# A transformer block in float32 on one core: the first feed-forward unit formed from seven block products, the first load in two transfers, the last output in columns of 384 and 128

## The chip, the core and the metric

The kernel runs on one core of one Trainium2 chip. The core has a matrix engine (PE, with its weight loads as PEld), a vector engine (DVE), a scalar engine (ACT), GpSimd (POOL) and a queue engine (SP) that only issues transfers. Each engine takes its own instructions in the order in which the built program holds them; engines wait for one another by semaphores. Matrix results go to PSUM, seven banks of 128 x 512 float32 that are used in rotation here (an eighth holds the attention output). The metric is the device time of one execution in microseconds, given as the median of some runs; a profiled execution has its own time, and its span runs from the first to the last instruction.

## The reference

For each of 8 batch entries there are 128 rows of 512 features (x) and 2048 context rows of 384 features. In short:

```
x = x + xattn(layernorm(x), ctx)              # 8 heads of 64; scores over 2048 context rows
h = layernorm(x)
q, k, v = h Wq + bq, h Wk + bk, h Wv + bv
x = x + h + (softmax over the query axis of (q k^T, causal) / sqrt(512)) v
h = layernorm(x)
hid = float8_e4m3(relu(h w1^T + b1))          # 512 -> 2048
x = x + float16(hid float8_e4m3(w2)^T + float16(b2))
```

## The kernel before, in words

**Stages.** The kernel first loads the first context block and the key weights and computes the keys of entry 0 by plain products (`k_plain`, L380), then goes through the eight entries of the cross-attention (keys and values by a scheme with fewer block products, scores, exponentials, transposition, weighted values), then the self-attention in two groups of four entries (`sa0`, `sa1`), and last the feed-forward part, also in two groups of 512 rows (`NG` = 2, `GT` = 512). It is the start, the passage from `sa1` to the feed-forward part, and the end that the change touches.

**Start.** Key weights arrive by six transfers on ACT's queue (L211), the first half of the first context block by six on SP's queue (L218): `n` picks 512 context rows, `k` one of three blocks of 128 features. Seven small products with the identity (L215, `early`) run on PE before any of it is there. Transfers of the two queues draw on eight semaphores in turn; a queue waits for the transfer that used the semaphore before.

**Feed-forward.** A hidden block is 128 hidden units for 512 rows. Computed directly (`hidden`, L1013), it takes four accumulating products (`k`) of 128 x 128 weights with 512 columns; in float32 each shows in the trace as two passes. `FourBlocks` (L1054) computes four hidden blocks at once from a 2 x 2 split of rows and features: seven block products in place of eight. It needs sums of weight blocks (`form_w`, L1034: t1, t2, t3, less_t4, two feature halves each, for a range of block pairs) and sums of row blocks (`form_x`, L1041: s1 to s4), both on DVE. `begin` holds products 1 and 2, `middle` 3 to 5, `end` 6 and 7; each `product` is eight passes with 256 columns. In the kernel before, hidden blocks 0 to 3 of group 0 are computed directly, one ahead of the last two `read` calls of the self-attention and three after them; seven `FourBlocks` units follow. The output (`output`, L1112, float8 weights; `finish`, L1119) of group 0 is put between the units of group 1; group 1's comes at the end, its last entry in two halves of 256 columns (L1189).

**What sets the order.** PE's order is written by hand for the whole kernel. ACT's and DVE's is written by hand up to L1155 and L1156 (`first.close()`, `in_turn.close()`): instructions emitted inside that region keep the order of the code. What is emitted after it (`form_x`, `form_w`, `quantize_w2` here) is placed by the build among the others, also ahead of them, by its own estimate of when operands are there.

**Weights w1.** One transfer of 4 MB on SP (L998), issued once the cross-attention's buffers are given up (L991) and the last `project` has been multiplied; the 16 transfers of `w2` (L1008, two buffers) stand behind it. All of w1 is one tile with one semaphore; `form_w` and the hidden products read it.

**The last steps of the self-attention** (L1128 to L1154), for `two` = entries 4 and 5 and then for 6 and 7: `values` is a product into a bank that DVE empties with the bias added (`sv`, L765); `logits` a product that DVE reads with the mask (`lg`, L735) and whose maximum it takes (`snm`, L739); `exps` an ACT step; `probabilities` two small DVE steps (`sr`, `e`); `keys` four products (`psk`) that ACT empties; `read` a product (`pr`) that DVE adds to the rows (L783). `turned_rows` transposes the normalized rows of group 0 on PE (`pt_f`) and copies them on ACT (`xf`).

Of the kernel before, what the change touches and what calls it, by code (L numbers as in the profile page):

```python
# [15 lines left out]
AF = mybir.ActivationFunctionType  # L16
# [4 lines left out]
P = 128  # L21
# [4 lines left out]
def tile_perceiver_block(  # L26
# [21 lines left out]
    nc = tc.nc  # L48
    B, S, D = x.shape
    _, DC, J = ctx_t.shape  # L50
# [5 lines left out]
    NK = D // P  # L56
    NKC = DC // P
    NJ = J // 512
    NJT = J // P
    NHC = HID // P  # L60
    NG = 2
    TMPB = 2
    BK = 256
    EARLY = 7
    GB = B // NG
    GT = GB * S
# [18 lines left out]
    def bank(name):  # L85
        return ps_one.tile([P, 512], F32, tag="bank", name=name)
# [3 lines left out]
    def turned_into(xt, b, xn, name):  # L90

        pt = bank(f"pt_{name}_{b}")
        for k in range(NK):
            nc.tensor.transpose(pt[:, ts(k, P)], xn[:, ts(k, P)], ident)
        nc.scalar.copy(xt[:, :, ts(b % GB, P)], pt.rearrange("p (k t) -> p k t", k=NK))
# [25 lines left out]
    x_both = ctxp.tile([P, 2, NKC, 4, BK], F32, tag="x_both", name="x_both")  # L121
# [91 lines left out]
    early = bank("early")  # L213
    for _ in range(EARLY):
        nc.tensor.matmul(early[:, :P], ident, ident, start=True, stop=True)  # L215
    for n in range(2):
        for k in range(NKC):
            nc.sync.dma_start(  # L218
                x_both[:, 0, k, 2 * n : 2 * n + 2],
                ctx_t[0, ts(k, P), ts(n, 512)].rearrange("p (i j) -> p i j", i=2),  # L220
            )
# [79 lines left out]
    wk4 = wk.rearrange("p k (f j n) -> p k f j n", f=2, j=2)  # L301
# [75 lines left out]
    def k_tile(b, f2):  # L377
        kts[b, f2] = ktp.tile([P, 2, J], F32, tag=f"kt{f2}", name=f"kt_{b}_{f2}")

    def k_plain(f2):  # L380


        k_tile(0, f2)
        for n in range(2):
            pss = [bank(f"k_{f2}_{j}_{n}") for j in range(2)]
            for k in range(NKC):
                for j in range(2):
                    nc.tensor.matmul(  # L388
                        pss[j], wk4[:, k, f2, j, :], x_both[:, 0, k, 2 * n : 2 * n + 2],
                        start=(k == 0), stop=(k == NKC - 1),  # L390
                    )
                if (n, k) == (1, 0):
                    yield
            for j in range(2):
                nc.scalar.copy(kts[0, f2][:, j, ts(n, 512)], pss[j])
# [268 lines left out]
    def load_columns(pool, src, name):  # L664
        t = pool.tile(list(src.shape), F32, tag=name, name=name)
        nc.gpsimd.dma_start(t, src)
        return t
# [118 lines left out]
    def all_of(unit):  # L786
        for _ in unit:
            pass
# [71 lines left out]
    def group_stats(g):  # L860

        st = small.tile([P, GB, 6], F32, tag="qst", name=f"fst_{g}")
        mv = small.tile([P, GB, 2], F32, tag="qmv", name=f"fmv_{g}")
        sd = small.tile([P, GB], F32, tag="qsd", name=f"fsd_{g}")
        for i in range(GB):
            nc.vector.bn_stats(st[:, i], xs[g * GB + i])
        for i in range(GB):
            nc.vector.bn_aggr(mv[:, i], st[:, i])
        nc.scalar.activation(sd, mv[:, :, 1], AF.Sqrt, bias=eps)
        return mv, sd  # L870

    def normed_group(g, mv, sd):
        rs = small.tile([P, GB], F32, tag="qrs", name=f"frs_{g}")
        nc.vector.reciprocal(rs, sd)
        out = []
        for i in range(GB):
            xn = sap.tile([P, D], F32, tag="xn", name=f"xn_f_{g}_{i}", bufs=GB + 1)
            nc.vector.tensor_scalar(
                xn, xs[g * GB + i], mv[:, i, 0:1], rs[:, i : i + 1], ALU.subtract, ALU.mult
            )  # L880
            out.append(xn)
        return out

    def turned_rows(g, rows, tag):

        xt = sap.tile([P, NK, GT], F32, tag=tag, name=f"xf_{g}")
        for i, xn in enumerate(rows):
            turned_into(xt, g * GB + i, xn, "f")
        return xt
# [107 lines left out]
    w1 = wff.tile([P, NK, HID], F32, tag="w1", name="w1")  # L997
    nc.sync.dma_start(w1, w1_t.rearrange("(k p) n -> p k n", p=P))  # L998
    b2r = load_row(wff, b2, "b2r")
    b1c = load_columns(wff, b1, "b1c")  # L1000
# [3 lines left out]
    def quantize_w2():  # L1004
        nc.vector.tensor_copy(b2q, b2r)
        for c in range(NHC):
            w = tp.tile([P, D], F32, tag="w2f", name=f"w2f_{c}", bufs=2)
            nc.sync.dma_start(w, w2_t[ts(c, P), :])  # L1008
            nc.vector.tensor_copy(w2[:, c, :], w, saturate=False)

    hq = wff.tile([P, NHC, B * S], E4M3, tag="hq", name="hq")

    def hidden(g, xt, blocks):  # L1013

        for c in blocks:
            ps = bank(f"ph_{g}_{c}")
            for k in range(NK):
                nc.tensor.matmul(  # L1018
                    ps, w1[:, k, ts(c, P)], xt[:, k, :], start=(k == 0), stop=(k == NK - 1)
                )  # L1020
            nc.scalar.activation(hq[:, c, ts(g, GT)], ps, AF.Relu, bias=b1c[:, c : c + 1], saturate=False)

# [4 lines left out]
    def b_of(k, j):  # L1030

        return w1.rearrange("p (q k) (c j n) -> p q k c j n", k=2, j=2, n=P)[:, :, k, :, j]

    def form_w(pairs):  # L1034
        t1, t2, t3, less_t4 = (w_forms[:, i, :, pairs] for i in range(4))
        b11, b12, b21, b22 = (b_of(k, j)[:, :, pairs] for k in range(2) for j in range(2))
        for q in range(2):
            for to, one, two in ((t1, b12, b11), (t2, b22, t1), (t3, b22, b12), (less_t4, b21, t2)):
                nc.vector.tensor_tensor(to[:, q], one[:, q], two[:, q], ALU.subtract)

    def form_x(g, xt):  # L1041
        a = xt.rearrange("p (q k) (i r) -> p q k i r", k=2, i=2)
        a11, a12, a21, a22 = (a[:, :, k, i] for i in range(2) for k in range(2))

        home, tag = ((sap, "sk"), (wff, "x_forms"))[g]
        f = home.tile([P, 4, 2, HR], F32, tag=tag, name=f"x_forms_{g}")
        s1, s2, s3, s4 = (f[:, i] for i in range(4))
        nc.vector.tensor_tensor(s1, a21, a22, ALU.add)
        nc.vector.tensor_tensor(s2, s1, a11, ALU.subtract)
        nc.vector.tensor_tensor(s3, a11, a21, ALU.subtract)  # L1050
        nc.vector.tensor_tensor(s4, a12, s2, ALU.subtract)
        x_forms[g] = a11, a12, a22, s1, s2, s3, s4
# [59 lines left out]
    def output(b, ps, blocks, cols=slice(0, D)):  # L1112
        for c in blocks:
            nc.tensor.matmul(  # L1114
                ps[:, cols], hq[:, c, ts(b, S)], w2[:, c, cols],
                start=(c == 0), stop=(c == NHC - 1),
            )

    def finish(b, ps, cols=slice(0, D)):  # L1119
        n = cols.stop - cols.start  # L1120
        q = tp.tile([P, n], E5M10, tag="q", name=f"q_{b}_{cols.start}", bufs=2)
        nc.vector.tensor_tensor(q, ps[:, cols], b2q[:, cols], ALU.add)
        y = sap.tile([P, n], F32, tag="xn", name=f"y_{b}_{cols.start}", bufs=GB + 1)
        nc.vector.tensor_tensor(y, q, xs[b][:, cols], ALU.add)
        nc.sync.dma_start(out[b][:, cols], y)
# [3 lines left out]
    sa1.scale(B - 1)  # L1129
    sa1.norm(B - 1)  # L1130
    nc.scalar.activation(warm, eps, AF.Exp)
    sa1.values(B - 2)

    sa1.logits(two[0])
# [6 lines left out]
        sa1.probabilities(r)  # L1141
    all_of(sa1.keys(sa1.rows[2:]))
    xfs = [turned_rows(0, xf0, "xt0")]
    for r in sa1.rows[2:]:
        sa1.logits(r)
        sa1.exps(r)
    for r in sa1.rows[2:]:
        sa1.probabilities(r)
    for r in two:
        sa1.read(r)  # L1150

    hidden(0, xfs[0], range(1))
    for r in sa1.rows[2:]:
        sa1.read(r)  # L1154
    first.close()  # L1155
    in_turn.close()  # L1156


    form_x(0, xfs[0])
    form_w(slice(2, 4))  # L1160
    hidden(0, xfs[0], range(1, 4))
    form_w(slice(4, 8))
    quantize_w2()
    form_w(slice(0, 2))
    work = [FourBlocks(0, d) for d in range(1, 4)] + [FourBlocks(1, d) for d in range(4)]
    work[0].begin()
    for i, unit in enumerate(work):
        if i == 1:
            xfs.append(turned_rows(1, normed_group(1, *group_stats(1)), "xt1"))
            form_x(1, xfs[1])  # L1170
        unit.middle()
        if i + 1 < len(work):
            work[i + 1].begin()
            unit.end()
        if i > 2:

            b = i - 3
            ps = bank(f"pf_{b}")
            output(b, ps, range(NHC))
            finish(b, ps)  # L1180
    unit.end()

    pss = [bank(f"pf_{b}") for b in range(GB, B - 1)]
    for b, ps in enumerate(pss, GB):
        output(b, ps, range(NHC - 4))
    for b, ps in enumerate(pss, GB):
        output(b, ps, range(NHC - 4, NHC))
        finish(b, ps)
    for i in range(2):  # L1189
        ps = bank(f"pf_{B - 1}_{i}")  # L1190
        cols = slice(i * D // 2, (i + 1) * D // 2)
        output(B - 1, ps, range(NHC), cols)
        finish(B - 1, ps, cols)

# [46 lines left out]
```

## Time and profile before

| | us |
|---|---|
| median of 3 runs (1086.44 to 1087.02) | 1086.88 |
| profiled execution | 1086.38 |
| its span | 1084.6 |
| PE busy in the span | 1077.8 |
| first `k_plain` pass begins | 4.98 |
| first direct hidden block begins on PE | 950.96 |
| first `FourBlocks` product begins | 966.41 |
| last output product begins its stretch of 80 passes | 1066.58 |

The page gives each engine's busy time and share; a timeline row gives start, duration, engine, line, operation, output tile <- input tiles, shape and count, and in brackets how long the engine stood idle before the row and what ended that. Rows of one line that follow each other are merged. The durations of products are longer than their distance, since passes are pipelined: eight passes with 256 columns are listed as 1.89 us but follow each other every 1.73 us.

### The profile page before, as it was taken

The numbers are of one execution on the slowest core, as the hardware profiler recorded it, in microseconds if no ns is written. First come the engines' busy times: TensorE is split into PE (matmuls) and PEld (weight loads), VectorE is DVE, ScalarE is ACT, GpSimd is POOL, SyncE is SP. The second block draws the span as 40 slices with busy tenths as digits, with TensorE's granted clock in tenths as the row PEclk, the third lists the DMA queues.
The fourth block names the chain that finished last, engine by engine and source line by source line (L and its number), as shares of the span: only waits on it lengthen the run. The fifth ranks groups of instructions, "written<-read, shape, count | busy, mean of one in ns | idle before, by whom it ended". The sixth has DMA issues, their size and how long they took to land.

```text
span 1084.6 us, 15566 instructions
## 1 busy us (share of the span) xinstructions
PE 1077.8 (99%) x5638; PEld 708.4 (65%) x5638; DVE 759.1 (70%) x1639; ACT 352.4 (32%) x559; POOL 234.4 (22%) x350
## 2 busy tenths in 40 slices
PE   9999999999999999999999999999999999999998
PEld 5475774576467647755775577557746656768875
DVE  5876567778777877787688777777877657584333
ACT  3322133324332423432343324332433222323221
POOL 0144130350055005500540153035000312000000
PEclk9999999999999999999999999999999999999999
DMA  9476334553565456536544553555345745431001
GB/s 324 141 188 151 119 78 98 136 147 85 131 155 134 93 136 152 138 87 150 149 100 100 154 146 78 117 137 146 79 112 115 233 122 146 175 106 31 10 17 52
DMA packets 71853, 134.75 MB, mean 124 GB/s; under 512 B 28241, under 2 KB 36449, under 8 KB 70753
## 3 DMA queue, kind: packets, MB, share of 16 engines
q1 hardware_dynamic: 61120, 113.03, 40.8%
q0 software_dynamic: 3312, 11.03, 3.3%
q10 hardware_dynamic: 7344, 9.70, 3.1%
q8 instruction: 45, 0.74, 0.3%
q14 instruction: 32, 0.25, 0.1%
HBM read 54.01 MB, written 10.49 MB: 59 GB/s over the span
## 4 chain that ended last, share of the span: by engine, by line
PE 99%; DMA 0%; ACT 0%; DVE 0%; issue 0%; ACTq 0%
PE pv_z L428 22%; PE pk_z L405 21%; PE po L559 11%; PE sc L504 11%; PE pv_b L428 4%; PE pk_b L405 3%; PE ph_b L1066 3%; PE psk L715 3%; PE psv L759 3%; PE pf L1114 3%; PE pq L472 3%; PE py L642 3%; PE ph_c L1066 2%; PE ph_a L1066 2%; PE k L388 2%; PE ph L1018 1%
## 5 line engine op out<-in xcount | busy, mean ns | idle before, releaser
L528 ACT ACTIVATE p<-p,nm 128x2048 f32<-128x2048 f32 x64 | 128.2, 2003 | 274.9 <-DVE nm L516 185.9
L541 DVE STREAM_TRANSPOSE p<-p 128x512 f32<-128x512 f32 x256 | 158.9, 679 | 62.3 <-ACT p L528 62.1
L508 DVE TENSOR_SCALAR_CACHE_REDUCE p<-sc 128x512 f32<-128x512 f32 x256 | 159.0, 686 | 20.6 <-PE sc L504 18.9
L428 PE MATMUL pv_z<-wv_sums,x_both 128*128 128x256 f32 x640 | 157.9, 381 | 0.0
L165 POOL TENSOR_TENSOR m_both<-x_both 128x256 f32<-128x256 f32 x70 | 51.0, 729 | 490.5 <-DMA x_both<-in_ctx_t_dram 303.1
L405 PE MATMUL pk_z<-x_both,wk_sums 128*128 128x512 f32 (+1 forms) x320 | 149.2, 572 | 1.1 <-ACT kt L325 0.6
L428 PEld LDWEIGHTS pv_z<-wv_sums,x_both 128*128 128x128 f32 x640 | 120.5, 190 | 18.6 <-issue 2.2
L559 PEld LDWEIGHTS po<-pT,v 128*64 128x64 f32 x2048 | 111.2, 137 | 23.9 <-issue 23.2
L559 PE MATMUL po<-pT,v 128*64 128x128 f32 x2048 | 118.9, 274 | 0.1
L504 PE MATMUL sc<-kt,q 64*128 64x512 f32 x512 | 118.5, 602 | 0.0
L428 PE MATMUL pv_z<-wv_sums,m_both 128*128 128x256 f32 x448 | 107.3, 379 | 0.0
L405 PEld LDWEIGHTS pk_z<-x_both,wk_sums 128*128 128x128 f32 x320 | 59.2, 190 | 67.3 <-issue 54.5
L405 PE MATMUL pk_z<-m_both,wk_sums 128*128 128x512 f32 (+1 forms) x224 | 101.4, 568 | 0.0
L428 PEld LDWEIGHTS pv_z<-wv_sums,m_both 128*128 128x128 f32 x448 | 83.4, 190 | 12.6 <-issue 0.6
L504 PEld LDWEIGHTS sc<-kt,q 64*128 64x128 f32 x512 | 46.9, 186 | 65.6 <-issue 54.7
L325 ACT COPY v<-pv_z 128x512 f32<-128x512 f32 x112 | 62.9, 589 | 56.0 <-PE pv_z L428 55.5
L325 ACT COPY kt<-pk_z 128x512 f32<-128x512 f32 (+1 forms) x112 | 59.7, 562 | 58.0 <-PE pk_z L405 57.6
L405 PEld LDWEIGHTS pk_z<-m_both,wk_sums 128*128 128x128 f32 x224 | 40.8, 190 | 46.8 <-issue 35.1
L165 POOL TENSOR_TENSOR x_both<-x_both 128x256 f32<-128x256 f32 x98 | 70.1, 731 | 2.4 <-DMA x_both<-in_ctx_t_dram 2.3
L328 DVE TENSOR_TENSOR v<-pv_z,v 128x512 f32<-128x512 f32 x96 | 63.1, 684 | 5.5 <-PE pv_z L428 5.5
L328 DVE TENSOR_TENSOR kt<-pk_z,kt 128x512 f32<-128x512 f32 (+1 forms) x96 | 59.9, 650 | 5.8 <-PE pk_z L405 5.4
L328 DVE TENSOR_TENSOR v<-pv_b,v 128x512 f32<-128x512 f32 x48 | 32.9, 686 | 40.4 <-PE pv_b L428 40.4
(208 smaller groups left out, 1235.7 us busy)
## 6 DMA issues: line engine op xcount, KB each, us to landing
pT<-p SPq DMA_DIRECT2D x488, 128.0 KB, 2.3
x_both<-in_ctx_t_dram SPq DMA_DIRECT2D x45, 512.0 KB, 5.2
w<-in_w_t_dram SPq DMA_DIRECT2D x1, 4096.0 KB, 12.9
w2f<-in_w_t_dram SPq DMA_DIRECT2D x16, 256.0 KB, 2.7
pT<-p POOLq DMA_DIRECT2D x24, 128.0 KB, 4.1
x_in<-in_x_dram SPq DMA_DIRECT2D x8, 256.0 KB, 7.2
qd<-xq SPq DMA_DIRECT2D x8, 256.0 KB, 2.6
q<-qd SPq DMA_DIRECT2D x8, 256.0 KB, 3.9
```

The lines of the kernel that those rows point to most:

```text
L165: eng.tensor_tensor(x_block(b, h, to), x_block(b, h, one), x_block(b, h, two), ALU.add if op == "+" else ALU.subtract,)
L325: nc.scalar.copy(outs[ij], views(ps))
L328: nc.vector.tensor_tensor(outs[to], views(ps), outs[other], op)
L405: nc.tensor.matmul(ps[:, : n * BK], wk_sums[:, WSLOT[WAT[r]], f2, :], x_block(b, hs, XAT[r]), start=start, stop=True, skip_group_check=True,)
L428: nc.tensor.matmul(ps[:, ts(t, 256)], x[:, ts(t, P)], wv_sums[:, WSLOT[WAT[r]], :], start=start and t == 0, stop=True, skip_group_check=True,)
L472: nc.tensor.matmul(ps, wq[:, k, ts(m, P)], xt[:, k, :], start=(k == 0), stop=(k == NK - 1),)
L504: nc.tensor.matmul(pair[i], q[r, :], kts[b, m // 2][r, m % 2, ts(n, 512)], start=True, stop=True)
L508: nc.vector.tensor_scalar(p[:, :, i].rearrange("p g (t i) -> p t g i", i=SQ)[:, ts(n, Q)], pair[i].rearrange("p (t g i) -> p t g i", g=Q, ...
L528: nc.scalar.activation(p[:, :, i], p[:, :, i], AF.Exp, bias=nms[b, m][:, i : i + 1], scale=SCALE, accum_out=sums[b][:, h : h + 1],)
L541: nc.vector.transpose(p[:, g, i], p[:, g, i])
L559: nc.tensor.matmul(pos[b][h * DH : (h + 1) * DH, ts(m, P)].rearrange("p (a i) -> p a i", a=Q), v[:, jt % 8, ts(2 * m + h, DH)], turned_[b, ...
L1066: nc.tensor.matmul(self.ps[to][:, ts(t, HR)], w[:, q, 2 * self.d + t], x[:, q], start=start and t == q == 0, stop=True, skip_group_check=True,
```

## The change

**1. First unit.** `hidden` is gone. All eight units of the two groups are `FourBlocks`. `form_w(slice(0, 2))` moves from behind `quantize_w2` to the place right after the `warm` activation, ahead of `sa1.values(B - 2)`; `form_x(0, ...)` moves from behind the closing of the region to right after `turned_rows`; the first unit's `begin` stands where hidden block 0 stood, between the two pairs of `read`. The other `form_w` calls and `quantize_w2` stay behind the region.

**2. First load.** The first context transfer (128 x 512) becomes two of 128 x 256, and the four passes of `k_plain` that read it become eight with 256 columns.

**3. Last output.** The last entry's columns are split 384 and 128 in place of 256 and 256.

```diff
-    for n in range(2):
-        for k in range(NKC):
+    for i in range(2):
+        nc.sync.dma_start(x_both[:, 0, 0, i], ctx_t[0, ts(0, P), ts(i, BK)])
+    for n in range(2):
+        for k in range(n == 0, NKC):
...
-                for j in range(2):
-                    nc.tensor.matmul(
-                        pss[j], wk4[:, k, f2, j, :], x_both[:, 0, k, 2 * n : 2 * n + 2],
-                        start=(k == 0), stop=(k == NKC - 1),
-                    )
+                for i in range(2 if f2 == n == k == 0 else 1):
+                    for j in range(2):
+                        to, of = slice(0, 512), slice(2 * n, 2 * n + 2)
+                        if f2 == n == k == 0:
+                            to, of = ts(i, BK), slice(i, i + 1)
+                        nc.tensor.matmul(
+                            pss[j][:, to], wk4[:, k, f2, j, :], x_both[:, 0, k, of],
+                            start=(k == i == 0), stop=(k == NKC - 1), skip_group_check=True,
+                        )
...
     nc.scalar.activation(warm, eps, AF.Exp)
+    form_w(slice(0, 2))
     sa1.values(B - 2)
...
     xfs = [turned_rows(0, xf0, "xt0")]
+    form_x(0, xfs[0])
...
-    hidden(0, xfs[0], range(1))
+    work = [FourBlocks(g, d) for g in range(NG) for d in range(NHC // 4)]
+    work[0].begin()
     for r in sa1.rows[2:]:
         sa1.read(r)
     first.close()
     in_turn.close()
-    form_x(0, xfs[0])
     form_w(slice(2, 4))
-    hidden(0, xfs[0], range(1, 4))
     form_w(slice(4, 8))
     quantize_w2()
-    form_w(slice(0, 2))
-    work = [FourBlocks(0, d) for d in range(1, 4)] + [FourBlocks(1, d) for d in range(4)]
-    work[0].begin()
...
-    for i in range(2):
+    for i, cols in enumerate((slice(0, D - P), slice(D - P, D))):
         ps = bank(f"pf_{B - 1}_{i}")
-        cols = slice(i * D // 2, (i + 1) * D // 2)
         output(B - 1, ps, range(NHC), cols)
```

The built programs differ on PE, DVE, ACT and SP at these places alone. DVE's order in the stretch, as built ("w" is one step of `form_w`, short with 256 columns and long with 512; "s" one of `form_x`; "cast" one block of `w2`; a number is the batch entry):

```
before: ... c_rows, sv6, lg4, snm4, lg5, snm5, sv7, sr4, e4, sr5, e5,
        8 w short, 4 w long, lg6, w long, snm6, lg7, s1, snm7, sr6, s2, e6, sr7, s3, e7,
        rows4, rows5, s4, 2 w long, rows6, rows7, w long, ...
after:  ... c_rows, 10 w short, sv6, lg4, w, snm4, lg5, w, snm5, sv7, sr4, w, e4, sr5, w, e5, 2 w,
        7 w long, s1, w long, s2, s3, s4, lg6, cast, snm6, lg7, cast, snm7, sr6, e6, sr7, e7,
        rows4, rows5, u2, rows6, rows7, ...
```

PE's order in the same stretch, with `psk` the key blocks of entries 6 and 7, and the PSUM banks as the build gave them: before, `psk` 2 takes the bank of `sv6`'s product and `psk` 3 that of `lg4`'s; after, `psk` 2 takes the bank of a transposition that ACT empties, `psk` 3 that of `sv6`'s product, and the four `pt_f` those of `lg4`, `lg5`, `sv7` and of `psk` 0.

```
before: psv6, pl4, pt_s7, pl5, psv7, psk 0-3, pt_f 0-3, pl6, pl7, pr4, pr5, hidden block 0, pr6, pr7, hidden blocks 1-3, ph_a ...
after:  psv6, pl4, pt_s7, pl5, psv7, psk 0-3, pt_f 0-3, pl6, pl7, pr4, pr5, ph_a, ph_b, pr6, pr7, ph_c ...
```

More of the change, by code (lines that the diff above doesn't have):

```diff
@@ L1011, in tile_perceiver_block @@
     hq = wff.tile([P, NHC, B * S], E4M3, tag="hq", name="hq")
[L1013 to L1021, printed above, removed]
     HR = GT // 2
@@ L1156, in tile_perceiver_block @@
     in_turn.close()
-    form_x(0, xfs[0])
     form_w(slice(2, 4))
-    hidden(0, xfs[0], range(1, 4))
     form_w(slice(4, 8))
     quantize_w2()
-    form_w(slice(0, 2))
-    work = [FourBlocks(0, d) for d in range(1, 4)] + [FourBlocks(1, d) for d in range(4)]
-    work[0].begin()
     for i, unit in enumerate(work):
-        if i == 1:
+        if i == 2:
             xfs.append(turned_rows(1, normed_group(1, *group_stats(1)), "xt1"))
@@ L1174, in tile_perceiver_block @@
             unit.end()
-        if i > 2:
-            b = i - 3
+        if i >= GB:
+            b = i - GB
             ps = bank(f"pf_{b}")
```

## The prediction

> **What bounds the kernel now.** I read the page's totals and its chain first, then the list of waits of PE alone, then the timelines of PE and DVE around the edit.
>
> ```profile
> span 1084.6 us, 15566 instructions
> ...
> PE 1077.8 (99%) x5638; PEld 708.4 (65%) x5638; DVE 759.1 (70%) x1639; ACT 352.4 (32%) x559; POOL 234.4 (22%) x350
> ...
> PE 99%; DMA 0%; ACT 0%; DVE 0%; issue 0%; ACTq 0%
> ```
>
> PE is busy for all but 6.8 us of the span, and those lie at the two ends (4.98 - 3.36 us before the first key pass, some 4 us after the last output pass). PE's waits name only two of 0.6 and 0.5 us in between. So PE work taken out shortens the kernel by its whole length, and any pause given to PE lengthens it by its whole length.
>
> ```profile
> 938.80 7.07 PE L715 MATMUL psk<-xt,both 128*128 128x256 f32 x32
> 945.71 1.91 PE L94 MATMUL pt_f<-ident,xn_f 128*128 128x128 f32 x16
> 947.45 1.95 PE L730 MATMUL pl<-xt,sk 128*128 128x128 f32 x16
> 949.24 1.88 PE L782 MATMUL pr<-sv,e 128*128 128x512 f32 x4
> 950.96 3.60 PE L1018 MATMUL ph<-xf,w 128*128 128x512 f32 x8
> 954.39 1.88 PE L782 MATMUL pr<-sv,e 128*128 128x512 f32 x4
> 956.11 10.46 PE L1018 MATMUL ph<-xf,w 128*128 128x512 f32 x24
> 966.41 1.89 PE L1066 MATMUL ph_a<-xf,w 128*128 128x256 f32 x8
> 968.13 1.89 PE L1066 MATMUL ph_b<-x_forms,w_forms 128*128 128x256 f32 x8
> ```
>
> The starts give the prices on PE: a direct hidden block 3.43 us (954.39 - 950.96), a `FourBlocks` product 1.73 us (968.13 - 966.41; 1.727 over the units), a key block 1.73, the four transpositions 1.74, two logits 1.79, two reads 1.72.
>
> ```profile
> 934.81 0.68 DVE L765 TENSOR_TENSOR sv<-psv,bv 128x512 f32<-128x512 f32 x1
> 935.41 0.34 DVE L735 SCALAR_TENSOR_TENSOR lg<-pl,c_rows,mask 128x128 f32<-128x128 f32 x1
> ...
> 939.00 0.69 DVE L765 TENSOR_TENSOR sv<-psv,bv 128x512 f32<-128x512 f32 x1 [2.36 <-PE psv L759]
> ...
> 943.06 0.76 DVE L1039 TENSOR_TENSOR w_forms<-w 128x256 f32<-128x256 f32 x2 [2.58 <-DMA w2f<-in_w_t_dram]
> ```
>
> This is the key view. Before, DVE finishes the softmax steps of entries 4 and 5 and only then waits for w1: the first `form_w` step begins at 943.06. The wait is put down to `w2f`, but w1 is what these steps read, and its issue row says the same: issued at 929.86, and
>
> ```profile
> w<-in_w_t_dram SPq DMA_DIRECT2D x1, 4096.0 KB, 12.9
> ```
>
> which is a landing at 942.8. The first `w2f` block was issued at 930.3 and took 13.1, too late to have ended the wait.
>
> **Part 1, what it saves.** Four direct blocks (4 x 3.43 = 13.73 us) go, seven products (7 x 1.727 = 12.09) come: -1.64 us of PE work. ACT's and DVE's extra evictions for the unit (one copy, eight short activations, four additions) run beside the products, as in the other seven units, which show PE without a pause.
>
> **Part 1, the wait that it adds.** `form_w(slice(0, 2))` now stands inside the hand-ordered region, right behind `c_rows`, which DVE reaches at 934.8. The transfer is issued as before, behind the last `project`, so DVE stands from 934.9 to 943.06. Queued behind the waiting step are `sv6`, `lg4`, `lg5`, `sv7` and everything after; waiting for those are PSUM banks. I follow them with durations of this trace (distance from start to start on DVE: short step 0.336, long step 0.60, `sv` 0.60, `lg` 0.27, `snm` 0.20, `sr` 0.09, `e` 0.20).
>
> First pause. Ten short steps come first: 943.06 + 10 x 0.336 = 946.42; `sv6` ends 0.68 later, 947.10. PE runs on unhindered through `psk` 0 to 2 (938.80 to 943.99); `psk` 3 needs the bank that `sv6` empties, and starts at 947.2 with 0.1 for the signal: **3.2 us** of pause.
>
> Second pause. From 947.2 PE has `psk` 3, transpositions, logits, reads and ph_a: 1.73 + 1.74 + 1.79 + 1.72 + 1.73 = 8.71, till 955.9. ph_b needs s2. DVE from 946.42: two `sv` 1.20, two `lg` and two `snm` 0.94, two `sr` and `e` 0.58, six short steps 2.02, eight long ones 4.82, s1 and s2 (with its end) 1.28: 10.84, so s2 is there at 957.26. Pause **1.4 us**; ph_b ends near 959.1. (ACT, behind DVE by its own queue, copies `xf` by 953, earlier than s1's turn.)
>
> Third pause. `read` 6 needs e6. After s2: s3, s4 1.2; `lg6`, cast, `snm6`, `lg7`, cast, `snm7` 1.6; then `sr6`, `e6` 0.4: near 960.4. PE could start at 959.1 and starts at 960.5: **1.4 us**. `read` 7 and e7 follow without a further wait. Before, the same DVE steps for 6 and 7 stood ahead of most `form_w` steps, and PE had a direct block (3.43 us, needing w1 and `xf` only) as cover; that cover is gone.
>
> Later, `u` steps stand among the casts of `w2`, which come only every 1.6 us because two buffers go round; I find 0.2 us there, once. Everything else has a product or more of slack. Each restart costs some 0.1 besides: in the start, after a stand at 12.33, two passes are 0.53 apart and not 0.43. Sum: 3.2 + 1.4 + 1.4 + 0.2 + 0.3 = 6.5 of pauses, less 1.64: **+4.9 us**.
>
> A rule to weigh here: the Trainium skill, "TensorE: Matmul & The Clock Gate" ("What's actually happening"), says the array falls back to half clock after about 3.4 us of idleness and needs as long again of work to come back. This trace shows a slower pace of PE only at the start: the early passes of 128 columns are 0.21 us apart, later ones of that width 0.11, and the first key pass takes 0.9 against 0.43. A pause of 3.2 us is just below the rule's window. By the rule at its worst, 3.4 us at half speed would cost 1.7 us of PE time, but between the first and third pause PE has 1.4 + 1.4 us to spare for it, since DVE sets the pace there. By row and by rule the sum stays +4.9.
>
> **Part 2.** The early passes keep PE busy to 4.6; the first key pass starts at 4.98, when the first weights (128 KB, issued 0.74, 4.2 us) and features (256 KB, 4.0 us) are in. Both share the transfer engines, so 128 KB less ahead saves some 0.3 us (256 KB and 128 KB arrive per 1.15 us in the next pair), but the passes gained run at the slower pace: gain 0.15. Columns and passes' total time are equal (8 of 256 for 4 of 512). The extra issue moves SP's queue by one, with its semaphores: the second half's first transfer now waits for the second weights (6.1 before, near 5.4 after, since less is ahead) and no longer for the first features (4.75), so it goes out some 0.5 us later. At 12.31 PE already waits 0.06 us for the transfer behind that one, which then took 6.2 us. It may land up to 0.4 later. Bounds: -0.35 (all hidden) to +1.6 (the slow landing hits the first transfer too, needed at 10.4); I take **+0.1**. The later x_in and wq transfers have over 2 us of slack.
>
> **Part 3.** Before, the last two runs of 16 passes with 256 columns take 0.109 us a pass. 384 columns cost 16 x 0.162 = 2.59. For 128 float8 columns with weights of their own the trace has no row. In proportion it is 0.055 (0.88 in all); the row of 128 float32 columns says 0.112 (1.79). The skill's page ("Back-to-back issue gap") gives 0.081 for load-and-multiply pairs with 128 columns, between the two: 1.30. Against 3.49 before, the sum is +0.40 by the page, 0 in proportion, +0.9 by the float32 row. On the other side the last two DVE steps shrink from 0.42 to some 0.29 each (512 columns 0.69, 256 0.42): -0.27, and the last transfer is half as large: -0.1. I take the page's price: **0.0**, from -0.2 to +0.6.
>
> **Sum.** +4.9 + 0.1 + 0.0 = +5.0 us. Profiled execution 1086.38 -> 1091.4, span 1084.6 -> 1089.6; the median lies 0.5 above this profiled execution, so the median is 1086.88 + 5.0 = **1091.9**. What a measurement of this kernel can tell from no change is about 0.2% (2.2 us).
>
> **Rivals.**
> (a) The wait reaches no bank that PE needs, or DVE catches up: PE keeps its -1.64 and the time is 1085.3, not slower. For it: DVE is busy only 70%. Against it: w1 cannot be earlier, 4 MB left at 929.86. Worked through the same sums, each microsecond of earlier landing takes one off until 940, then the two later pauses go; break-even is a landing near 938.3, 4.5 us before the measured one.
> (b) Only the first pause counts, since DVE's queue behind it empties faster than summed: 3.2 + 0.1 - 1.64 = +1.7: 1088.6. For it: the second and third pause are differences of long sums. Against: DVE is listed busy 11.9 of the 12.2 us from 943.9 to 956.1 already before, and six short and three long steps more now stand ahead of e6.
> (c) The start loses as well, up to its bound: 1091.9 + 1.5 = 1093.4.
>
> **Chances.** The forecast 0.71 (its own range 1090.5 to 1093.0), (a) 0.06, (b) 0.10, (c) 0.13. Slower by over 0.2% means above 1089.05: the forecast, (c) and a part of (b), 0.88; within 0.2% the rest of (b) and most of (a), 0.10; faster 0.02. Range for 8 in 10: 1089.2 to 1094.0, which leaves out (a), half of (b) and little at the top.
>
> **What would show it.** In the changed profile: DVE idle some 8.2 us ahead of the first `w_forms` step, which still begins near 943; PE's waits with new rows, `psk` <- DVE `sv` near 3.2, ph_b <- `x_forms` near 1.4, `pr` <- `e` near 1.4; PE's busy time lower by 1.6 while the span grows by 5; the last units still 12.1 us apart plus output. The forecast is wrong if PE shows no wait at `psk`, if w1 lands well before 943, or if the first key passes show a wait above 1 us.

## The result and the profile after

The changed kernel takes 1089.8 us (median of 11 runs, 1089.02 to 1090.46), the kernel before 1086.61 beside it: +3.2 us, a ratio of 1.003 with a 95% interval of 1.0022 to 1.0038. The profiled execution has a span of 1088.0 against 1084.6, +3.4. The sign, the place and the mechanism are as predicted; the size is 1.8 us smaller than the +5.0 of the sum. The time lies in the prediction's range for 8 in 10 (from 1089.2), but below the forecast's own range (from 1090.5).

The page of the changed kernel, its totals and the shares of its chain:

```profile
span 1088.0 us, 15636 instructions
...
PE 1077.1 (99%) x5666; PEld 713.3 (66%) x5666; DVE 762.5 (70%) x1644; ACT 353.4 (32%) x564; POOL 234.5 (22%) x350
...
PE 77%; DVE 2%; DMA 1%; SPq 1%; ACT 0%; issue 0%; DVEq 0%; ACTq 0%
```

PE's busy time hardly moved while the span grew, and DVE and DMA, with 0% of the chain before, now have a share of it. (The listed chain begins at 195 us, so its shares don't add up to 100%; the 77% is not a loss of PE time.) In the passage it leaves PE for the issue of w1 at 929.8, runs through the transfer and DVE's steps, and comes back to PE at the read of entry 6, at 960.07. The list of PE's waits names where (columns: total, times, longest):

```profile
PE psk L722 <- DVE sv L772: 2.7, 1, 2.7
...
PE pr L789 <- DVE e L760: 1.2, 1, 1.2
PE ph_b L1063 <- DVE x_forms L1046: 1.2, 1, 1.2
```

These three rows are new, and no other is. In PE's timeline of the passage each stands before its product (in brackets the idle time and its releaser):

```profile
938.77 5.34 PE L722 MATMUL psk<-xt,both 128*128 128x256 f32 x24
946.77 1.99 PE L722 MATMUL psk<-xt,both 128*128 128x256 f32 x8 [2.65 <-DVE sv L772]
948.60 1.91 PE L94 MATMUL pt_f<-ident,xn_f 128*128 128x128 f32 x16
...
953.85 1.89 PE L1063 MATMUL ph_a<-xf,w 128*128 128x256 f32 x8
956.90 1.97 PE L1063 MATMUL ph_b<-x_forms,w_forms 128*128 128x256 f32 x8 [1.16 <-DVE x_forms L1046]
960.07 1.96 PE L789 MATMUL pr<-sv,e 128*128 128x512 f32 x4 [1.21 <-DVE e L760]
961.87 1.89 PE L1063 MATMUL ph_c<-x_forms,w_forms 128*128 128x256 f32 x8
963.59 1.89 PE L1063 MATMUL ph_a<-xf,w 128*128 128x256 f32 x8
```

By distances of starts: from 938.77 to 963.59 are 24.82 us; the products in it need 19.08 (four key blocks 6.92, transpositions 1.74, logits 1.79, four reads 3.44, three products 5.19). The rest, **5.7 us**, is pause: 2.8 ahead of `psk` 3, 1.3 ahead of `ph_b`, 1.4 ahead of read 6, 0.2 in restarts. DVE's timeline shows what each waited for:

```profile
934.72 0.14 DVE L644 TENSOR_TENSOR c_rows<-c_rows,both_biases 128x1 f32<-128x1 f32 x1
942.67 0.76 DVE L1036 TENSOR_TENSOR w_forms<-w 128x256 f32<-128x256 f32 x2 [7.81 <-DMA w2f<-in_w_t_dram]
...
946.04 0.68 DVE L772 TENSOR_TENSOR sv<-psv,bv 128x512 f32<-128x512 f32 x1
...
956.08 0.68 DVE L1046 TENSOR_TENSOR x_forms<-x_forms,xf 128x512 f32<-128x512 f32 x1
...
959.64 0.28 DVE L760 TENSOR_SCALAR e<-e,sr 128x128 f32<-128x128 f32 x1
```

The stand of 7.81 us is again put down to `w2f`, but w1 is what these steps read; it was issued at 929.83, and its issue row is

```profile
w<-in_w_t_dram SPq DMA_DIRECT2D x1, 4096.0 KB, 12.6
```

DVE stands from 934.9 to 942.67, then does ten short steps, then `sv6`, whose end at 946.72 lets `psk` 3 start; s2 ends at 956.76 and `ph_b` starts at 956.90; e6 ends at 959.92 and the read starts at 960.07.

The whole of +3.4: pauses 5.7, products -1.64, the way up to 938.8 nothing (938.77 against 938.80), the end -0.7 (below).

### The profile page after: what moved, and what is told of

The parts are those of the page before. It is cut to its first block, busy times and chain, and to the rows that moved or that the text cites. A ratio compares the mean times of both kernels' runs of the same rounds, so it can differ in the third digit from the quotient of the medians.

```text
span 1088.0 us, 15636 instructions
## 1 busy us (share of the span) xinstructions
PE 1077.1 (99%) x5666; PEld 713.3 (66%) x5666; DVE 762.5 (70%) x1644; ACT 353.4 (32%) x564; POOL 234.5 (22%) x350
## 4 chain that ended last, share of the span: by engine, by line
PE 77%; DVE 2%; DMA 1%; SPq 1%; ACT 0%; issue 0%; DVEq 0%; ACTq 0%
PE pv_z L435 17%; PE pk_z L412 16%; PE po L566 9%; PE sc L511 9%; PE ph_b L1063 4%; PE pv_b L435 3%; PE pk_b L412 3%; PE ph_c L1063 3%; PE py L649 3%; PE pf L1111 2%; PE ph_a L1063 2%; PE psk L722 2%; PE psv L766 2%; DMA w2f<-in_w_t_dram 1%; DVE w_forms L1036 1%; SPq L554 1%
## 5 line engine op out<-in xcount | busy, mean ns | idle before, releaser
L435 PEld LDWEIGHTS pv_z<-wv_sums,m_both 128*128 128x128 f32 x448 | 83.4, 190 | 12.9 <-POOL x_both L165 0.5
## 6 DMA issues: line engine op xcount, KB each, us to landing
w<-in_w_t_dram SPq DMA_DIRECT2D x1, 4096.0 KB, 12.6
```

The costliest lines, as they stand in the source:

```text
L435: nc.tensor.matmul(ps[:, ts(t, 256)], x[:, ts(t, P)], wv_sums[:, WSLOT[WAT[r]], :], start=start and t == 0, stop=True, skip_group_check=True,)
```

## Experiments

Each is compared with the kernel before, run on the same chip at the same time: 1086.1 us in the first two groups, 1086.44 in the last. Where a few tenths matter, spans and rows of the profile are used.

**The first part alone.** The changed kernel with the first load and the last output as before.

> The kernel before with the first part of the change alone (all eight units of seven products, form_w(0:2) ahead of the softmax steps); first load and last output as before. My theory: all of the loss is made here, by three pauses of PE in the passage to the feed-forward part (2.8, 1.3 and 1.4 us and some 0.2 for the restarts, by distances of starts in the changed kernel's trace: 5.7) less 1.64 us of products: +4.1 us, 1090.7. The changed kernel's +3.2 is then +4.1 and about -0.6 to -0.9 from the other two parts. Rival: the end's shorter time in the changed profile was chance, the other parts are worth nothing, and this one gives +3.2 to +3.5, 1089.8 to 1090.1.

Measured: 1090.49, +4.4 us (interval of the ratio 1.0024 to 1.0049); span +4.1. The interval, +2.6 to +5.3 us, holds the rival's +3.2 to +3.5 too, so the time does not decide; the profile does. PE's waits are the same three, of 2.7, 1.2 and 1.2, and the end of the span is as in the kernel before (3.1 us behind the last `y`, table below). So the loss is made here, and its size is the one summed from the changed kernel's trace.

**The third part alone.**

```diff
-    for i in range(2):
+    for i, cols in enumerate((slice(0, D - P), slice(D - P, D))):
         ps = bank(f"pf_{B - 1}_{i}")
-        cols = slice(i * D // 2, (i + 1) * D // 2)
```

> The kernel before with the third part alone (last entry's columns 384 and 128). My theory, from the two profiles: the last DVE step ends 0.10 us earlier beside PE's progress, and the last transfer, half as large, is in 0.5 us sooner: -0.6 us, 1086.0. Rival: the last transfer's 2.07 against 1.57 us was a difference between single executions: -0.1 to 0, 1086.5.

Measured: 1086.06, against 1086.08 before: no difference (0.9991 to 1.0007). The rival is nearer. In the profile the last `y` step ends 1081.29 against 1081.51, and from there to the end of the span it is 2.9 us against 3.1: a gain of 0.2, and not the 0.6 seen in the changed kernel. Something else in that kernel shortens its end.

**The second and third part.**

> The kernel before with the second and third part (first features in two transfers; columns 384 and 128), the first feed-forward unit as before. My theory: the start gains 0.2 to 0.35 us at the first key pass, and PE's later waits at fixed times give most of it back, as in the changed profile where +0.1 to -0.03 us is left from 217 us on: as the third part alone, within 0.2 us: 1085.8 to 1086.0. Rival: the start's gain stays: 0.25 us less than the third part alone. Second rival: the second half's transfer comes late, and the start costs up to 1 us: 1087.

Measured: 1085.58, -0.5 us (0.9985 to 1.0001, so not told from nothing). The start gives nothing that can be told: at PE's transpositions near 22.8 us, the eight profiled kernels with the first features in two transfers stand from 0.5 us earlier to 0.4 later than the kernel before, and four others with the old start from 0.4 earlier to 0.5 later. The first key pass does begin earlier in all eight (4.5 to 4.6, against 4.9 to 5.1 in the five with the old start). The late transfer of the second rival shows in this profile as a wait of PE for `x_both` of 0.8 us, and yet the transpositions stand at 22.88 against 22.78. The end of the span is here 2.5 us behind the last `y`, as in the changed kernel.

**The end by itself.** Both runs leave all of the computation as before; entry 0's output transfer, some 60 us ahead of the end, is cut in two or three.

```diff
-        nc.sync.dma_start(out[b][:, cols], y)
+        cuts = (0, 256, 512) if b == 0 else (0, n)
+        for lo, hi in zip(cuts, cuts[1:]):
+            nc.sync.dma_start(out[b][:, cols.start + lo : cols.start + hi], y[:, lo:hi])
```

> The kernel before with the output transfer of entry 0, in the middle of the feed-forward part, cut in two of 256 columns; nothing else. From the traces so far: eight semaphores serve SP's and ACT's transfers in turn, and at the end SP waits for all eight one after the other; from the end of the last y step to the end of the span it took 3.1 us where the last transfer had the seventh semaphore (the kernel before, and the first part alone; 2.9 with the third part's smaller transfer), 2.5 us where it had the eighth (all kernels with both the second and third part), 3.3 where it had the first (both kernels with w1 in two transfers). My theory: the turn of the semaphores decides this, so one more transfer anywhere moves the last one to the eighth: 3.1 - 0.4 = 2.7 us here, with the last transfer still of 128 KB. Rival: the shorter end came from the third part alone: 3.1 stays.

> As the run with one more transfer, but entry 0's output goes in three (128, 128 and 256 columns), so that the last transfer of the kernel comes to the first semaphore of the row. My theory: the seven other waits now stand behind it: 3.1 + 0.4 = 3.5 us from the last y step to the end of the span. Rival: the count of transfers has no effect: 3.1.

The last row of DVE's timeline in the kernel before (span 1084.6), and SP's waits for output transfers at the end (columns: total, times, longest):

```profile
1081.09 0.42 DVE L1124 TENSOR_TENSOR y<-q,rows 128x256 f32<-128x256 f16 x1
...
SPq L1237 <- DMA out_dram<-y: 0.9, 1, 0.9
```

The same with one more transfer, and the page's first row:

```profile
span 1083.8 us, 15568 instructions
...
1080.78 0.42 DVE L1124 TENSOR_TENSOR y<-q,rows 128x256 f32<-128x256 f16 x1
...
SPq L1239 <- DMA out_dram<-y: 0.4, 1, 0.4
```

and with two more:

```profile
span 1084.4 us, 15571 instructions
...
1080.51 0.42 DVE L1124 TENSOR_TENSOR y<-q,rows 128x256 f32<-128x256 f16 x1
...
SPq L1239 <- DMA out_dram<-y: 1.2, 1, 1.2
```

From the end of `y` to the end of the span: 1084.6 - 1081.51 = 3.1 before, 1083.8 - 1081.20 = 2.6 with one more, 1084.4 - 1080.93 = 3.5 with two (their times, 1085.7 and 1086.17, are one execution each and can't tell 0.4 us). By the issue rows, SP's and ACT's queues issue 663 transfers in the kernel before, 8 x 82 + 7, so that the last one has the seventh semaphore. With all the kernels:

| kernel | last transfer | its semaphore of the eight | `y` to end of span, us |
|---|---|---|---|
| before; first part alone | 128 KB | seventh | 3.1; 3.1 |
| third part alone | 64 KB | seventh | 2.9 |
| second and third part; changed | 64 KB | eighth | 2.5; 2.5 |
| one more transfer | 128 KB | eighth | 2.6 |
| two more transfers | 128 KB | first | 3.5 |
| w1 in two transfers (below) | 64 KB | first | 3.3 |

The turn decides. At the end SP waits for the eight semaphores one after the other, and each wait takes time though its transfer is long in (0.06 to 0.09 us, one of them 0.36, in the trace's list of SP's instructions). In the kernel before and in both runs SP's wait for the last transfer ends 1.72 us after that transfer's issue; the waits that still stand behind it take 0.44 us before (one is left), 0.07 with one more (none) and 0.84 with two more (seven). The changed kernel's end gained 0.4 us because its **start** issues one transfer more.

**form_w(0:2) behind the softmax steps.** The one line goes back to where DVE waited for w1 before.

```diff
     nc.scalar.activation(warm, eps, AF.Exp)
-    form_w(slice(0, 2))
     sa1.values(B - 2)
...
     for r in two:
         sa1.probabilities(r)
+    form_w(slice(0, 2))
```

> The changed kernel with one line moved: form_w(0:2) stands behind the probabilities of entries 4 and 5, where DVE waited for w1 in the kernel before. My theory: the first pause (2.8 us) goes wholly, since sv 6 no longer queues behind w1's landing; s2 ends near 951.8, ahead of PE's need at 952.7, so the second (1.3) goes too; e6 comes near 955.4 against a need at 954.4, since some long form_w steps still stand ahead of it: about 1.0 us of the third is left. 1086.6 - 1.64 - 0.7 + 1.0 = 1085.3. Rival: the pauses come from the amount of DVE work that the unit needs before ph_b and the second read, wherever it stands: the first goes, the other two (2.8) stay, and the time is 1087.1.

Measured: 1085.44, -0.6 us (0.9986 to 1.0002); span 1083.5. First and second pause are gone, and the row that is left, with DVE's timeline ahead of it:

```profile
PE pr L789 <- DVE sr L759: 1.1, 1, 1.1
```

```profile
953.38 0.34 DVE L742 SCALAR_TENSOR_TENSOR lg<-pl,c_rows,mask 128x128 f32<-128x128 f32 x1
953.64 0.68 DVE L1036 TENSOR_TENSOR w_forms<-w,w_forms 128x512 f32<-128x512 f32 x1
954.24 0.28 DVE L746 TENSOR_REDUCE snm<-lg 128x1 f32<-128x128 f32 x1
954.44 0.15 DVE L759 RECIPROCAL sr<-sden 128x1 f32<-128x1 f32 x1
954.51 0.67 DVE L1036 TENSOR_TENSOR w_forms<-w 128x512 f32<-128x512 f32 x1
955.10 0.28 DVE L760 TENSOR_SCALAR e<-e,sr 128x128 f32<-128x128 f32 x1
```

One line's place is worth 4.5 us of span (3.8 by the medians, each beside its own run of the kernel before). The long steps of `form_w(4:8)`, which the build put between the small steps, each push e6 back by 0.6; that is the pause that stays.

**w1 in two transfers.** Here the hand-written order of DVE ahead of `sv6` stays, and the data comes earlier: the 512 columns of the first unit go first.

```diff
-    nc.sync.dma_start(w1, w1_t.rearrange("(k p) n -> p k n", p=P))
+    for cols in (slice(0, HID // 4), slice(HID // 4, HID)):
+        nc.sync.dma_start(w1[:, :, cols], w1_t.rearrange("(k p) n -> p k n", p=P)[:, :, cols])
```

> The changed kernel with w1 in two transfers: the 512 columns of the first unit (1 MB), then the rest (3 MB). The order of DVE ahead of sv 6 stays (form_w(0:2) first); only the landing of what it reads is earlier, by about 9 us. My theory (DVE stands for w1's landing): no first pause, since the steps run from 934.9 or soon after and sv 6 is done before 940; second pause gone; at e6 some 0.8 us, since the other form_w steps still wait for the rest near 942.8 and stand ahead of e6. 1085.1. Rival: it is the place in the order and not the transfer that costs: no gain, 1089.8.

Measured: 1085.96, -0.15 us (0.9989 to 1.0005); span 1084.1, 3.9 less than the changed kernel. DVE's timeline has no stand ahead of `sv6`:

```profile
934.65 0.15 DVE L644 TENSOR_TENSOR c_rows<-c_rows,both_biases 128x1 f32<-128x1 f32 x1
934.93 0.42 DVE L1037 TENSOR_TENSOR w_forms<-w 128x256 f32<-128x256 f32 x1
...
937.86 0.68 DVE L772 TENSOR_TENSOR sv<-psv,bv 128x512 f32<-128x512 f32 x1
```

So the place alone costs nothing; place and landing together do. (Eight short steps stand ahead of `sv6` here, not ten: the build had put two steps of `form_w(2:4)` among them in the changed kernel, and puts them later here. By their distance of 0.336 each, the two make up 0.7 us of the first pause.) DVE's stand for the rest of w1, 1.20 us up to 942.28, holds up nothing that PE waits for. A wait of 0.9 for e6 is left, as expected; the 0.8 us that the expectation missed is the end, where the additional transfer puts the last one on the first semaphore (3.3 against 2.5).

**The long steps held.** `form_w(4:8)` is written behind the last reads; `form_w(0:2)` stays early.

```diff
     for r in sa1.rows[2:]:
         sa1.read(r)
+    form_w(slice(4, 8))
     first.close()
...
-    form_w(slice(4, 8))
     quantize_w2()
```

> The changed kernel with form_w(4:8), eight steps of 0.60 us, written into the hand-ordered region behind the last reads, so that the build can't place them ahead of s2 and e6; form_w(0:2) stays ahead of the softmax steps. My theory: the first pause (2.8) stays; s2 and e6 come 4.8 us less some casts earlier, so the second and third (1.3 and 1.4) go: 1089.8 - 2.8 = 1087.0, at most 0.5 more if the casts of w2 that move up wait for their transfers. Rival: the later pauses are only the first one handed on, and stay: 1089.8.

Measured: 1088.77, +2.7 us (1.0014 to 1.0032); the expectation, some 0.4 over the kernel before, is missed. The second pause fell to 0.2 (`ph_b` starts 955.43 - 953.52 = 1.91 us behind `ph_a`), the first is listed with 2.3, since w1 landed 0.3 earlier, and the third stayed:

```profile
PE pr L789 <- DVE e L760: 1.5, 1, 1.5
```

```profile
950.33 0.75 DVE L1016 CAST w<-w2f 128x512 fp8e4<-128x512 f32 x2
953.32 0.43 DVE L1016 CAST w<-w2f 128x512 fp8e4<-128x512 f32 x1 [2.24 <-DMA w2f<-in_w_t_dram]
953.66 0.68 DVE L1045 TENSOR_TENSOR x_forms<-xf 128x512 f32<-128x512 f32 x1
```

The build filled the place with casts of w2, and the third of them stands 2.24 us for a transfer whose buffer had only just been given back. The bound of 0.5 put on that was wrong. The run neither shows that the later pauses come from the long steps nor that they don't; the next one does.

**Both moves.**

> The changed kernel with both moves: form_w(0:2) behind the probabilities of entries 4 and 5, and form_w(4:8) behind the last reads. My theory: no pause of PE is left in the passage: 1086.6 - 1.64 - 0.7 = 1084.2, faster than both kernels. Rival: the long steps, now later, stand ahead of the second unit's additions and give 1 to 2 us back there: 1085.5.

Measured: 1084.0 us, a ratio of 0.9979 to the kernel before (0.9971 to 0.9987), -2.1 us: faster than both. All that is left in PE's list of waits lies in the first 100 us:

```profile
PE early L215 <- POOL ident masks.py:199: 1.5, 1, 1.5
PE pk_z L412 <- ACT kt L328: 0.6, 1, 0.6
PE k L395 <- DMA x_both<-in_ctx_t_dram: 0.3, 1, 0.3
PE pk_z L412 <- DVE kt L334: 0.3, 1, 0.3
```

It differs from the run with one line moved only by the long steps, and the pause at e6 is gone: they had made it. (Casts of w2 take some of their places, and shift e6 less.)

**w1 later, by much and by little.** A part of w1 is loaded once more ahead of it (the 1 MB of its first 128 features, or 64 KB), and w1 starts when that is in. "The rule" of the two expectations is the one that the prediction weighs, of the Trainium skill, "TensorE: Matmul & The Clock Gate" ("What's actually happening").

```diff
+    nc.sync.dma_start(w1[:, 0], w1_t[ts(0, P), :])
     nc.sync.dma_start(w1, w1_t.rearrange("(k p) n -> p k n", p=P))
```

The run with 64 KB has `w1[:, 0, :P]` and `w1_t[ts(0, P), :P]` in the added line.

> The changed kernel with w1's first quarter (1 MB) loaded once more ahead of w1, into the same place, so that w1 starts behind it and lands some 4 to 5 us later. The result is the same. My theory: the first pause grows by the whole delay (2.8 to about 7 us), the two later ones stay as they are, as DVE sets the pace between: 1089.8 + 4.0 to 5.0 = 1093.8 to 1094.8. Rival: after a pause this long PE restarts at half clock for about 3.4 us as the rule says: key block psk 3 takes 3.4 us instead of 1.8, hidden by the second pause at first (1.3 us to spare), so up to 0.4 more, and the granted clock or the distance of passes shows it. Second rival: the 1 MB does not delay w1 much (same queues, no wait): under 3.3 us.

> The changed kernel with a small transfer (64 KB, into a part of w1 that w1 itself then fills again) ahead of w1, which starts when that is in: some 2 us later. The result is the same. My theory: the first pause grows from 2.7 to 4.7 us. In the run with w1 5.4 us later, PE stood for 8.3 us and then ran at a granted clock of 0.50 for some 4.9 us; in the changed kernel it stood for 2.7 and kept 1.00. By the rule (3.4 us of idleness) a pause of 4.7 brings the half clock as well: psk 3 takes 3.6 us instead of 1.8, the later pauses shrink to 0.2 to 0.3, and the time is that of the changed kernel + 2.0 to 2.3. Rival: the clock falls only after a longer stand, psk 3 takes 1.8, the later pauses stay at 1.2: the same + 2.0, so the time does not tell these two apart, but the granted clock does.

Measured: 1096.02 (+9.9 us; 1.0072 to 1.0103) and 1093.92 (+7.5; 1.0053 to 1.0086), both more than expected. The `form_w` steps begin at 948.05 and 945.49, 5.4 and 2.8 later than in the changed kernel, and PE stands 8.3 and 5.3 us at `psk` 3. Then it runs slowly. Windows of PE with 1 MB ahead (columns: stretch and its length, PE busy and passes, granted clock, share of DMA, GB/s):

```profile
944.10:946.70 2.60, 0.00 (x0) 1.00 0.99 408
...
946.90:952.10 5.20, 0.00 (x0) 0.50 0.09 33
952.15:957.00 4.85, 4.85 (x14) 0.50 0.00 2
...
957.20:958.20 1.00, 1.00 (x12) 1.00 0.00 0
```

with 64 KB ahead:

```profile
944.30:949.40 5.10, 0.00 (x0) 1.00 0.19 74
...
949.60:952.80 3.20, 3.20 (x8) 0.50 0.01 3
...
953.00:956.50 3.50, 3.50 (x33) 1.00 0.00 0
```

and in the changed kernel itself:

```profile
944.20:946.70 2.50, 0.00 (x0) 1.00 0.00 0
946.77:950.20 3.43, 3.43 (x23) 1.00 0.01 2
```

So a longer stand does bring half the clock, and the changed kernel was spared it. In the run with 64 KB, `psk` 3 takes 953.03 - 949.59 = 3.44 us instead of 1.83. The account of that run against the changed kernel: pause +2.7, half clock +1.6, second pause -1.3, third -0.3, the end +0.9 (the last transfer on the first semaphore again), the start +0.2: 3.8, and the spans differ by 3.7. With 1 MB: pause +5.6, half clock 1.8 at `psk` 3 and 0.7 at the transpositions, second pause -1.3, third -1.1, end +0.8, start -0.2: 6.3 against 6.2. The half clock cost next to nothing in either: 2.5 us lost and 2.4 got back from the two later pauses with 1 MB, 1.6 and 1.6 with 64 KB. What the expectations missed is the size of the delay (a pause 5.6 longer and not 4.0 to 5.0, 2.7 and not 2.0) and the end (+0.8 and +0.9).

## Why the prediction was right, and where its size was off

- **PE sets the time; products -1.64.** Right: from the fourth product of the new unit (963.59, behind all pauses) to the last stretch of output products (1070.67) the changed kernel needs 107.08 us; the one before needs 100.17 from the start of its first unit (966.41 to 1066.58). The difference, 6.91, is the four products of 1.727 that were left of the new unit.
- **First pause, predicted 3.2, measured 2.8.** The chain was right (w1, ten short steps, `sv6`, the bank of `psk` 3), and each step lasted what was said. w1 took 12.6 us instead of 12.9, so the steps began 0.4 earlier. This is scatter between executions, not a step of the argument: from w1's issue to the first step it took 12.5 to 13.3 us in the ten profiles that load w1 as the kernel before does, and the sum leaned on one of them (13.2). That `w1` is the cause is shown from both sides: with data earlier the pause is gone, with data 2.8 and 5.4 later it is 2.7 and 5.6 longer.
- **Second and third pause, 1.4 each, measured 1.3 and 1.4.** Right, and so is their cause: what stands ahead of s2 and e6 in DVE's queue. The third needs the long steps, by the two runs that differ in them alone.
- **The later 0.2 (`u` among the casts) and 0.3 for restarts.** The first did not come; restarts cost 0.2.
- **The clock.** The changed kernel's pause left it at 1.00. The argument that DVE sets the pace, so that half clock would be paid out of the later pauses, held where it could be seen: with 64 KB ahead, 1.6 lost at `psk` 3 and 1.6 less in the two pauses; with 1 MB, 2.5 lost and 2.4 less.
- **Part 2, +0.1.** Not told from nothing, within its bounds. Rival (c), a late landing at the start, appears in four of the eight profiles with the new start, and in none of the five with the old one, as a wait of PE for `x_both` of 0.3 to 0.8 us; by 22.8 us the start's spread is as large without it. The earlier first pass came (0.36 us, 4.62 against 4.98 in the changed kernel), and what is left of it can't be told from the spread.
- **Part 3 and the end, 0.0; this is the step that failed, by 0.7.** Two terms of it. First, the price of a 128-column pass: the estimate weighed 0.112, 0.081 and 0.055 us and took 0.081. In the trace the first of the 16 passes begins at 1083.625 and the last at 1084.463, 0.056 apart, the share by columns. DVE's timeline behind them:

```profile
1083.83 0.56 DVE L1119 TENSOR_TENSOR q<-pf,b2q 128x384 f16<-128x384 f32 x1 [0.51 <-PE pf L1111]
1084.42 0.56 DVE L1121 TENSOR_TENSOR y<-q,rows 128x384 f32<-128x384 f16 x1
1084.90 0.28 DVE L1119 TENSOR_TENSOR q<-pf,b2q 128x128 f16<-128x128 f32 x1
1085.21 0.29 DVE L1121 TENSOR_TENSOR y<-q,rows 128x128 f32<-128x128 f16 x1
```

The figure of the Trainium skill, "TensorE: Matmul & The Clock Gate" ("Back-to-back issue gap"), 0.081 for a load and multiply pair with 128 columns, does not hold for these float8 passes; the measurement decides. With 0.056 the prediction's own sum gives -0.3 at the last `y`. Measured is -0.1: from the first output product of the last stretch to the end of the last `y` it is 1085.50 - 1070.67 = 14.83 us against 14.93. The sum also had the wrong engine in the path there. The last `q` shows no wait for PE; it stands behind `y` of the 384 columns, so that DVE's four steps lead to the end. (At 0.081 a pass PE would have ended some 0.2 us behind that `q`'s start, by estimate: 15 x 0.025 = 0.4 later than its 1084.7, against 1084.90.)

The smaller transfer gives 0.1 to 0.2 (1.6 us to landing in the page's issue row against 1.7; 2.9 against 3.1 us from `y` to the end).

Second, the turn of the end's semaphores, -0.4, which the sum did not have: the prediction counted part 2's additional issue where it stands, and not at the end of the count.

Pauses 0.8 smaller, an end 0.7 shorter and the start's 0.1 make the 1.6 us by which the span's +3.4 falls short of +5.0; the medians lie 0.2 closer together still, which is inside their spread.

## What to carry over

A step that waits for a transfer costs nothing where its engine would stand anyway, and its whole wait where an in-order queue holds the release of another engine's buffers behind it: look for the last place in the queue ahead of which everything the pacing engine needs is done, and move the step there, or make the piece of the transfer that it needs smaller. What a build may place freely it also places between the steps of a chain that is late (long additions first, casts that wait for transfers when those were taken away), so hold it behind that chain by hand. And when transfers are added or taken away, the last one's turn among the semaphores moves, which here was worth -0.4 to +0.4 us at the end.

## What was not expected of the hardware

The end of the span depends on how many transfers the kernel has issued before, with nothing changed near the end: 2.6, 3.1 and 3.5 us behind the last step for three neighbouring counts.

The granted clock did not follow the stand by a fixed delay: by the windows above and finer ones it fell at 946.9, some 3.0 us after PE's last pass, in one run, and at 949.5, 5.2 us after it, in the other, and stayed at half for 10.2 and 3.4 us. The Trainium skill, "TensorE: Matmul & The Clock Gate" ("What's actually happening"), speaks of a free-running window of 3.4 us that must be idle; three such windows and one fit both lengths, and a window that runs freely fits the two delays, but for the first, which is some 0.4 us short of a whole idle window. If that is so, a pause of 2.8 us like the changed kernel's is not far from the edge; a length in between was not tried.
